# Norm statistics without transposes in a two-layer graph attention kernel

## The chip, the cores and the metric

The kernel runs on one core of one Trainium2 chip. The metric is the device time of one execution in microseconds (us); the times of the kernel before are the median, the lowest and the highest of three runs. Profiles come from one further execution each, whose own time is given beside the span of its profile.

## The reference, cut to what matters

64 graphs of 256 tokens with 512 features and a dense 256 x 256 weight matrix `adj` each go through three attentions, one after the other. All of it is float32.

```python
# layer 0: 8 heads
Q, K, V = x @ W_q + b_q, x @ W_k + b_k, x @ W_v + b_v
scores = QK/8 + a[:, :, None] + c[:, None, :] + log(adj + 1e-9)   # a, c = x @ w_g halves
x = softmax(scores) @ V + x
# layer 1, twice: 8 heads with W1, then 1 head with W2
y = (x - mean) * rsqrt(var + 1e-6) * g + b                        # the layer norm
h = y @ W;  s, t = h @ a_src, h @ a_dst
e = leaky_relu(s[:, None] + t[None, :], 0.2) + adj
x = softmax(e) @ h + x
```

The two layer norms need, for every token, the mean and the variance over its 512 features. That is what the change touches.

## The kernel before

**Layout.** One graph is one chain of some 40 steps. Its activations stand turned: `xT`, `yT` and `zT` are tiles of 128 partitions x 4 chunks x 256 tokens, so that the features of a token lie along the partitions and the chunks. `xT` is the input, `yT` the result of the first attention (with its residual), `zT` that of the second. The norm is folded into the weights (`fold_norm`): the mean is taken out of W1 and W2 beforehand, and only the factor 1/sqrt(var + eps), `rstd`, is applied per token, as TensorE's products are evicted (L607, L614, L616).

**The steps of a graph**, by the names that the order lists use:

- "load": DMA of X (L454, four pieces) and A. "turn": VectorE turns X into `xT` by 32 x 32 blocks (L471), and `adj` into AT; GpSimd forms four sums of quarters of `xT` (`left_factors`, L282 to L285, tile S); `xT` is stored to DRAM.
- "V", "V7", "V4", "Q", "Q7", "Q4", "K", "K7", "K4": a product of two 2 x 2 blocked matrices with seven block products instead of eight (`winograd`, L306 and L313). Banks a, b, c of PSUM are refilled: a product on a used bank waits for the eviction of what was in it (ScalarE L495, L528, L607; VectorE L507, L537, L545, L616).
- "scores": QK (L562) and the exponential on ScalarE (L569). "mask": VectorE multiplies by AT (L583) and adds two halves (L588).
- "sums 0": TensorE sums the weights with 32-column strips (L362), VectorE takes the reciprocal (L368), it goes to DRAM and comes back spread over the partitions as R (L376). "product 0": weights times V (L394). "gather 0": VectorE multiplies by R (L403) and adds bias and residual (L408), which gives `yT`; GpSimd forms S from it.
- "tokens 1": the statistics of `yT`, see below. "V1", "V1 7", "V1 4": the product with W1. "rows 1": the rows for the second attention go through DRAM and come back as R (L433, L443).
- "weights", eight times: ScalarE L647, VectorE L650; then the total L655. "sums 1", "product 1", "gather 1": as above, and give `zT`.
- "tokens 2": the statistics of `zT`, and the residual: X2, `zT` turned back so that tokens lie along the partitions, plus a row of biases (GpSimd L669). "V2", "V2 7", "V2 4", "rows 2", "weights 2" (L694, L699), "product 2" twice (L711, L716, L718), and the result goes to `out` (L727).

**The statistics (`tokens`, `rstd_of`).** For each half of 128 tokens TensorE transposes four 128 x 128 blocks into one bank of PSUM (L249). ScalarE reads it with Identity and adds it up (L264), scales the total by -1/512 (L265), and squares the difference, adding up again (L266). VectorE turns the sum of squares into the variance (L270), and GpSimd raises it to -1/2 (L272):

```python
for t, pt in tokens(xT):                      # 4 transposes on TensorE per half
    nc.scalar.activation(to, pt, AF.Identity, accum_out=total[:, of])
    nc.scalar.mul(less[:, of], total[:, of], -1.0 / D)
    nc.scalar.activation(pt, pt, AF.Square, bias=less[:, of], accum_out=squares[:, of])
```

For `zT` the first pass of ScalarE writes not into PSUM but into X2, which is how the residual gets turned.

**What sets the order.** TensorE's order is written out by hand: the list `period` has 42 steps, each with the age of the graph that it belongs to, so six graphs are under way at once; the lists `start` and `finish` replace the first and the last repetitions. The order of the emitted steps is TensorE's program order. The other engines' instructions are placed by a scheduler that sees the same steps; once placed, each engine works through its row in order, and so does SP, which issues nearly all DMAs. Tiles come from pools: PSUM is a ring of eight banks, ET (the weights) has four buffers, S of `yT` and of `zT` share one buffer ("yS"), X has one.

**The weights' preparation.** `fold_norm` multiplies W1 and W2 with the attention vectors on GpSimd (L177, tile `product`, which takes ET buffers) and adds up on VectorE (L181), during the first graphs.

## Time and profile before

| | us |
|---|---|
| median of three runs (lowest, highest) | 3304.04 (3301.4, 3307.49) |
| the profiled execution, its own time | 3304.79 |
| span of its profile | 3303.0 |
| TensorE matmul busy | 3208.0 |
| TensorE weight load busy | 2686.9 |
| VectorE busy | 2488.2 |
| ScalarE busy | 1761.0 |
| GpSimd busy | 899.5 |
| ScalarE's squares, L266, and their reads | 165.8 and 49.9 |
| ScalarE's first pass, L264, both forms, and its reads | 150.2 and 49.8 |
| ScalarE's scaling, L265 | 43.5 |
| TensorE's transposes, L249, all forms | 137.4 |

How to read it: PE is TensorE's matmul, PEld its weight load, DVE VectorE, ACT ScalarE, POOL GpSimd, SP the engine that issues DMAs. Busy times of a group are the union of its instructions; matmuls are pipelined and overlap, so the price of a group of matmuls is better read from the distance between the starts of two groups in the timeline than from its length. A float32 product is recorded as two matmuls, a transpose as one. A line of the timeline has the start, the length, the engine, the source line, the operation with the tile written and the tiles read, and the number of merged instructions. A line of the waits has who waited, for whom, the total, the number and the longest, in us. The granted clock of TensorE was 0.991 of full speed over the span.

### The profile page before, as it was taken

The page shows a single profiled execution, that of the slowest core. Times are in us where ns is not written, and L with a number is a line of the kernel's source. Part 1 is how long each engine was busy: PE and PEld are TensorE (multiplying, and loading weights), DVE is VectorE, ACT ScalarE, POOL GpSimd, SP SyncE. Part 2 cuts the span into 40 slices and gives each one's busy share as a digit, 9 for nine tenths or more (in the row PEclk, how much of TensorE's full clock was granted, in tenths as well). Part 3 has the DMA queues.
Part 4 walks back from the last instruction along what each step waited for, and adds up shares of the span by engine and source line. Part 5 has one row for each costly group of instructions (what it writes and reads, how often), then busy time and mean ns, then how long its engine had stood idle before and what let it go on. Part 6 is the DMA issues. An engine that isn't in the chain of part 4 may idle for free.

```text
span 3303.0 us, 76975 instructions
## 1 busy us (share of the span) xinstructions
PE 3208.0 (97%) x29000; PEld 2686.9 (81%) x29000; DVE 2488.2 (75%) x5267; ACT 1761.0 (53%) x4807; POOL 899.5 (27%) x1244
## 2 busy tenths in 40 slices
PE   6899999999999999999999999999999999999997
PEld 4688888888888888888888888888888888888875
DVE  4667777777777777787777777777777777777775
ACT  2455555555555555555555555555555555555553
POOL 2222222322322322322322322322222222222222
PEclk8999999999999999999999999999999999999998
DMA  4324333333333333343343343343343333333322
GB/s 121 105 80 112 106 97 104 109 103 104 106 107 103 105 108 103 97 115 102 98 116 101 97 112 104 93 116 104 93 118 100 98 113 105 98 107 110 99 91 69
DMA packets 271656, 340.91 MB, mean 103 GB/s; under 512 B 108577, under 2 KB 187569, under 8 KB 271281
## 3 DMA queue, kind: packets, MB, share of 16 engines
q1 hardware_dynamic: 270512, 335.40, 36.1%
q8 instruction: 232, 3.80, 0.5%
q14 instruction: 144, 1.17, 0.1%
q10 hardware_dynamic: 768, 0.54, 0.1%
HBM read 233.48 MB, written 102.31 MB: 102 GB/s over the span
## 4 chain that ended last, share of the span: by engine, by line
PE 80%; ACT 10%; DVE 3%; DMA 3%; issue 2%; SPq 1%; POOL 1%; ACTq 0%; DVEq 0%; POOLq 0%
PE ps_a L306 18%; PE ps_num L394 12%; PE ps_a L313 10%; PE ps_b L306 9%; PE ps_sc L562 7%; PE ps_av L711 6%; ACT ET L647 6%; PE ps_c L306 4%; PE ps_su L362 4%; PE ps_b L313 3%; PE ps_tr L249 3%; ACT m L528 2%; DMA R<-kept 2%; PE ps_c L313 2%; ACT u L528 1%
## 5 line engine op out<-in xcount | busy, mean ns | idle before, releaser
L650 DVE SCALAR_TENSOR_TENSOR ET<-R,f,ET 128x256 f32<-128x256 f32 x1024 | 468.3, 496 | 243.4 <-ACT ET L647 214.7
L647 ACT ACTIVATE ET<-AT,lift 128x256 f32<-128x256 f32 x1024 | 442.6, 505 | 172.0 <-PE ps_num L394 172.0
L394 PE MATMUL ps_num<-ET,V 128*32 128x256 f32 x8192 | 466.6, 380 | 0.0
L394 PEld LDWEIGHTS ps_num<-ET,V 128*32 128x32 f32 x8192 | 264.0, 110 | 155.1 <-issue 1.3
L583 DVE TENSOR_TENSOR ET<-ET,AT 128x1024 f32<-128x1024 f32 x256 | 305.2, 1227 | 112.3 <-ACT ET L569 112.3
L569 ACT ACTIVATE ET<-ps_sc,V 128x512 f32<-128x512 f32 x512 | 303.1, 702 | 101.5 <-PE ps_sc L562 90.2
L380 POOL TENSOR_TENSOR added<-added,inverse 128x128 f32<-128x128 f32 x128 | 60.1, 470 | 891.7 <-DVE inverse L368 891.7
L306 PE MATMUL ps_a<-w,S 128*128 128x264 f32 (+1 forms) x1024 | 278.6, 395 | 9.0 <-ACT m L607 8.7
L306 PE MATMUL ps_b<-w,S 128*128 128x264 f32 (+1 forms) x1024 | 267.0, 383 | 0.1
L711 PE MATMUL ps_av<-V,ET 128*128 128x258 f32 (+1 forms) x1024 | 246.6, 385 | 5.7 <-DVE ET L699 5.7
L306 PEld LDWEIGHTS ps_a<-w,S 128*128 128x128 f32 x1024 | 183.4, 190 | 71.9 <-ACT m L607 24.8
L562 PE MATMUL ps_sc<-QT,KT 64*128 64x256 f32 x2048 | 240.0, 384 | 0.0
L562 PEld LDWEIGHTS ps_sc<-QT,KT 64*128 64x128 f32 x2048 | 193.7, 188 | 41.5 <-issue 20.9
L282 POOL TENSOR_TENSOR S<-yT 128x256 f32<-128x256 f32 x64 | 54.5, 851 | 626.2 <-PE ps_su L362 556.9
L306 PEld LDWEIGHTS ps_b<-w,S 128*128 128x128 f32 x1024 | 193.9, 189 | 31.5 <-issue 0.5
L711 PEld LDWEIGHTS ps_av<-V,ET 128*128 128x128 f32 x1024 | 187.1, 193 | 29.1 <-issue 4.6
L272 POOL TENSOR_TENSOR rstd<-var,mhalf 128x2 f32<-128x2 f32 x128 | 90.6, 708 | 284.7 <-DVE var L270 278.2
L282 POOL TENSOR_TENSOR S<-zT 128x256 f32<-128x256 f32 x63 | 45.8, 727 | 445.5 <-DVE zT L408 419.2
L403 DVE TENSOR_TENSOR ps_num<-ps_num,R 128x512 f32<-128x512 f32 x256 | 165.1, 690 | 1.7 <-DMA R<-kept 1.0
L266 ACT ACTIVATE ps_tr<-ps_tr,less 128x512 f32<-128x512 f32 x256 | 165.8, 648 | 0.1
L306 PE MATMUL ps_a<-wv,xT 128*128 128x257 f32 x512 | 142.2, 400 | 22.0 <-ACT ET L569 11.6
L669 POOL TENSOR_TENSOR X<-X,bw 128x512 f32<-128x512 f32 x128 | 159.6, 1267 | 5.7 <-ACT X L264 5.7
(167 smaller groups left out, 7022.8 us busy)
## 6 DMA issues: line engine op xcount, KB each, us to landing
R<-kept SPq DMA_DIRECT2D x128, 512.0 KB
X<-in_x_dram SPq DMA_DIRECT2D x256, 128.0 KB
kept<-xT SPq DMA_DIRECT2D x64, 512.0 KB
yT<-kept SPq DMA_DIRECT2D x64, 512.0 KB
R<-kept SPq DMA_DIRECT2D x512, 64.0 KB
kept<-yT SPq DMA_DIRECT2D x64, 512.0 KB
out_dram<-X SPq DMA_DIRECT2D x512, 64.0 KB
zT<-kept SPq DMA_DIRECT2D x63, 512.0 KB
```

Of the source, the lines that this page charges most:

```text
L266: nc.scalar.activation(pt, pt, AF.Square, bias=less[:, of], accum_out=squares[:, of])
L306: nc.tensor.matmul(to, A[:, kk, :], B[:, kk, :], start=(first and kk == 0), stop=(kk == 1), skip_group_check=not first,)
L313: nc.tensor.matmul(to[:, m * P : (m + 1) * P], B[:, kk, m * P : (m + 1) * P], A[:, kk, :], start=(first and m == kk == 0), stop=(kk == 1), ...
L394: nc.tensor.matmul(num[32 * a : 32 * a + 32, m * N : (m + 1) * N], V[:, j, a // 2, a % 2 * P + q * DH + 32 * m :][:, :32], pair[a // 2][:, ...
L403: nc.vector.tensor_tensor(both, both, R[:, q, :].unsqueeze(1).to_broadcast([P, 2, N]), ALU.mult)
L562: nc.tensor.matmul(banks[h % 2][:, o : o + N], KT[lo : lo + DH, (q + h) // 2, j * P : (j + 1) * P], QT[lo : lo + DH, (q + h) // 2, :], sta ...
L569: nc.scalar.activation(ET[:, j, i::2, :], banks[i].rearrange("p (h n) -> p h n", n=N), AF.Exp, bias=c[:, j, :],)
L583: nc.vector.tensor_tensor(ET[:, j, :, :], ET[:, j, :, :], AT[:, j, :].unsqueeze(1).to_broadcast([P, 4, N]), ALU.mult,)
L647: nc.scalar.activation(ET[:, j, h, :], AT[:, j, :], AF.Exp, bias=lift[:, j, at : at + 1])
L650: nc.vector.scalar_tensor_tensor(ET[:, j, h, :], R[q][:, h, :], f[:, j, at : at + 1], ET[:, j, h, :], ALU.max, ALU.mult,)
L669: nc.gpsimd.tensor_tensor(X2[t], X2[t], folded["2"].row, ALU.add)
L711: nc.tensor.matmul(av[:, :width], ET[:, j, t * P : (t + 1) * P], V2[:, j, n, :width], start=(j == 0), stop=(j == NT - 1),)
```

## The change

Three things are changed together.

1. The statistics no longer go through transposes. ScalarE squares the whole tile (`squares_of`), GpSimd adds the four chunks of the squares and of the values in two steps each, and TensorE multiplies with a tile of ones, four 32-column strips of 128 partitions, so that sums over the partitions come out; VectorE turns them by 32 x 32 blocks, and computes the variance from the sum and the sum of squares. A tile `skew` keeps a measure of how much the two cancel, checked once at the end. The squares use the buffer of S before S is formed.
2. The residual X2 is turned by VectorE (tile Z, in the buffer of X), stored to DRAM and read back in eight pieces; then GpSimd adds the row as before.
3. The lists `period`, `start` and `finish` are new. `product` of `fold_norm` moves from the buffers of ET to those of R, `sums` and `bad` to those of "kept", and half of the loads of W_q go to ScalarE's queue.

```diff
-        def tokens(xT):
-            for t in range(NT):
-                pt = ps("tr")
-                for kc in range(KC):
-                    nc.tensor.transpose(
-                        pt[:, kc * P : (kc + 1) * P], xT[:, kc, t * P : (t + 1) * P], ident
-                    )
-                yield t, pt
...
+        def squares_of(xT, tag):
+            S = data.tile([P, 4, 2, P], F32, name="S", tag=tag)
+            wide = S.rearrange("p i k n -> p (i k n)").rearrange("p (k n) -> p k n", k=KC)
+            sums = small.tile([P, 2, N], F32, name="sums", tag="stats", bufs=1)
+            nc.scalar.activation(wide, xT, AF.Square)
+            for i, (v, half) in enumerate(((xT, wide[:, 2:]), (wide, wide[:, :2]))):
+                if i == 0:
+                    nc.gpsimd.tensor_tensor(wide[:, :2], wide[:, :2], wide[:, 2:], ALU.add)
+                    nc.gpsimd.tensor_tensor(half, v[:, :2], v[:, 2:], ALU.add)
+                nc.gpsimd.tensor_tensor(sums[:, i], half[:, 0], half[:, 1], ALU.add)
+            return S, sums
...
+        def rstd_of(sums, n):
+            pt = ps("st")
+            for g in range(4):
+                nc.tensor.matmul(
+                    pt[32 * g : 32 * g + 32, :P], all_ones,
+                    sums.rearrange("p i (t g r) -> p g i t r", t=NT, g=4)[:, g],
+                    start=True, stop=True,
+                )
+            turned = small.tile([P, 2, NT, 32], F32, name="turned", tag="turned", bufs=1)
+            nc.vector.transpose(turned.rearrange("p i t r -> p (i t r)"), pt[:, :P])
+            total, squares = turned[:, 0, :, 0], turned[:, 1, :, 0]
+            square = small.tile([P, NT], F32, name="square", tag="square")
+            nc.vector.tensor_tensor(square, total, total, ALU.mult)
             var = small.tile([P, NT], F32, name="var", tag="var")
-            nc.vector.tensor_scalar(var, squares, 1.0 / D, 1e-6, ALU.mult, ALU.add)
+            nc.vector.scalar_tensor_tensor(var, square, -1.0 / D, squares, ALU.mult, ALU.add)
+            nc.vector.scalar_tensor_tensor(skew[:, n], var, -16.0 * D, square, ALU.mult, ALU.add)
+            nc.vector.tensor_scalar(var, var, 1.0 / D, 1e-6, ALU.mult, ALU.add)
             rstd = small.tile([P, NT], F32, name="rstd", tag="rstd")
             nc.gpsimd.tensor_tensor(rstd, var, mhalf.to_broadcast([P, NT]), ALU.pow)
...
-            left = left_factors(xT, "yS")
+            S, sums = squares_of(xT, "yS")
+            left = left_factors(xT, "yS", S)
             stored = store(xT)
             yield
-            rstd = rstd_of(xT)
+            rstd = rstd_of(sums, b)
...
-            X2 = [
-                data.tile([P, D], F32, name="X2", tag="X2", bufs=4) for t in range(NT)
-            ]
-            rstd = rstd_of(xT, lambda t: by_chunk(X2[t]))
+            rstd = rstd_of(sums, B + b)
+            Z = data.tile([P, 2 * KC, P], F32, name="Z", tag="X")
+            nc.vector.transpose(
+                Z.rearrange("p b (k r) -> p k b r", k=KC), xT.rearrange("p k (b r) -> p k b r", r=32)
+            )
+            kept = dram.tile([P, 2 * KC, P], F32, name="kept", tag="keptz")
+            nc.sync.dma_start(out=kept, in_=Z)
+            X2 = data.tile([P, NT, D], F32, name="X2", tag="X2", bufs=2)
+            for q in range(4):
+                for t in range(NT):
+                    nc.sync.dma_start(
+                        out=X2[32 * q : 32 * q + 32, t, :].rearrange("r (a f) -> r a f", a=4),
+                        in_=kept.rearrange("(a r) (t q) f -> t q r a f", a=4, t=NT)[t, q],
+                    )
...
         period = [
-            (2, "rows 1"), (1, "mask"), (0, "V"), (0, "V7"), (4, "V2 4"), (1, "sums 0"),
-            (2, "weights"), (1, "product 0"), (1, "gather 0"), (4, "rows 2"), (4, "weights 2"),
-            (0, "V4"), (3, "weights"), (0, "Q"), (3, "weights"), (0, "Q7"), (3, "sums 1"),
-            (3, "product 1"), (2, "weights"), (2, "weights"), (-1, "load"), (1, "tokens 1"),
-            (0, "Q4"), (3, "gather 1"), (4, "product 2"), (2, "weights"), (1, "V1"), (2, "weights"),
-            (-1, "turn"), (1, "V1 7"), (0, "K"), (3, "tokens 2"), (0, "K7"), (4, "product 2"),
-            (0, "K4"), (1, "V1 4"), (2, "weights"), (3, "V2"), (0, "scores"), (0, "scores"),
-            (3, "V2 7"), (0, "mask"),
+            (4, "tokens 2"), (5, "product 2"), (1, "scores"), (0, "V"), (2, "rows 1"),
+            (1, "mask"), (3, "weights"), (4, "V2"), (0, "V7"), (3, "weights"),
+            (4, "V2 7"), (1, "mask"), (3, "weights"), (1, "sums 0"), (2, "weights"),
+            (1, "product 0"), (4, "V2 4"), (3, "weights"), (4, "rows 2"),
+            (3, "weights"), (0, "V4"), (1, "gather 0"), (0, "Q"), (3, "sums 1"),
+            (2, "weights"), (3, "product 1"), (2, "weights"), (0, "Q7"),
+            (4, "weights 2"), (-1, "load"), (4, "product 2"), (1, "tokens 1"),
+            (0, "Q4"), (1, "V1"), (-1, "turn"), (1, "V1 7"), (0, "K"), (3, "gather 1"),
+            (0, "K7"), (1, "V1 4"), (0, "K4"), (0, "scores"),
         ]
...
-            load_weight(nc.sync, wq, W_q)
+            load_weight(nc.sync, wq, W_q, range(0, 2))
+            load_weight(nc.scalar, wq, W_q, range(2, KC))
...
+        note_odd(skew.rearrange("p n t -> p (n t)"), -3.0e38, 0.0)
```

## The prediction

> **What bounds the kernel now.** I read the busy shares first, then the stretches of the run, then one repetition of the step list in the timeline, engine by engine, and last the waits of the start. The busy shares (part 1 of the page) and two stretches of 1000 us, with PE, PEld, DVE, ACT and POOL busy in that order:
>
> ```profile
> PE 3208.0 (97%) x29000; PEld 2686.9 (81%) x29000; DVE 2488.2 (75%) x5267; ACT 1761.0 (53%) x4807; POOL 899.5 (27%) x1244
> ...
> 1000.00:2000.00 1000.00, 994.17 (x9051) 836.97 (x9049) 769.07 (x1622) 549.98 (x1502) 274.99 (x382) 1.00 0.38 105
> 2000.00:3000.00 1000.00, 995.36 (x9067) 838.13 (x9068) 768.86 (x1622) 551.11 (x1503) 273.71 (x380) 1.00 0.37 104
> ```
>
> TensorE is the bound: it is idle 0.6% of the middle. Next is VectorE with 77%. TensorE's timeline gives the length of a period and the prices (start, length, then the group):
>
> ```profile
> 1504.70 1.03 PE L306 MATMUL ps_a<-wv,xT 128*128 128x257 f32 x4
> ...
> 1510.86 1.08 PE L362 MATMUL ps_su<-total,ones 128*32 128x128 f32 x32
> 1511.76 3.64 PE L394 MATMUL ps_num<-ET,V 128*32 128x256 f32 x64
> ...
> 1526.67 1.09 PE L249 MATMUL ps_tr<-ident,yT 128*128 128x128 f32 x8
> 1527.60 1.06 PE L313 MATMUL ps_a<-xT,wq 128*128 128x128 f32 x8
> ...
> 1540.08 1.04 PE L249 MATMUL ps_tr<-ident,zT 128*128 128x128 f32 x8
> 1540.96 1.06 PE L313 MATMUL ps_a<-S,wk 128*128 128x128 f32 x8
> ...
> 1554.42 1.03 PE L306 MATMUL ps_a<-wv,xT 128*128 128x257 f32 x4
> ```
>
> The same step comes back after 1554.42 - 1504.70 = 49.72 us: one graph per period. Ends overlap the next start, so a group costs the distance to the next start: 0.93 and 0.88 us for the two transposes, 0.90 for the 32 strips of L362.
>
> VectorE and GpSimd in the same period:
>
> ```profile
> 1512.40 0.92 DVE L368 RECIPROCAL inverse<-ps_su 128x128 f32<-128x128 f32 x1
> ...
> 1520.30 1.29 DVE L403 TENSOR_TENSOR ps_num<-ps_num,R 128x512 f32<-128x512 f32 x2
> 1521.50 1.65 DVE L408 SCALAR_TENSOR_TENSOR yT<-ps_num,columns,yT 128x256 f32<-128x256 f32 x4
> ...
> 1543.59 1.10 DVE L270 TENSOR_SCALAR var<-squares 128x2 f32<-128x2 f32 x1
> ...
> 1546.81 0.72 DVE L345 TENSOR_TENSOR top<-top,ends 128x32 f32<-128x32 f32 x1
> ```
> ```profile
> 1542.16 2.50 POOL L669 TENSOR_TENSOR X<-X,bw 128x512 f32<-128x512 f32 x2
> ...
> 1546.72 0.76 POOL L283 TENSOR_TENSOR S<-S,xT 128x256 f32<-128x256 f32 x1
> ```
>
> See two things. VectorE takes the reciprocal 0.6 us after the sums begin to leave TensorE, and yT is done at 1523.15, 3.5 us before its transposes: slack. And L270 on two columns takes 1.10 us, L345 0.72 (their fast instances take 0.15): each ends when the GpSimd instruction beside it ends. The start has one long idle, two links of the waits:
>
> ```profile
> ACT ET L569 <- DVE w L181: 11.3, 1, 11.3
> PE ps_a L306 <- ACT ET L569: 11.6, 1, 11.6
> ```
>
> **What the Trainium skill says.** "SBUF — State Buffer", Who interferes with whom: a VectorE instruction with two SBUF inputs and a GpSimd instruction that reads SBUF share one read port, and whichever starts second blocks until the first ends. The trace agrees (L270, L345; L699 beside L282 takes 0.96 us for 0.48). "TensorE: Matmul & The Clock Gate", Part 3: matmuls on different column strips run at once. The trace agrees: 32 strip records of L362 take 0.90 us, as 8 full-width records do. The same page, Part 1: after about 3.4 us of idleness the clock halves. The trace agrees: after 4.06 us idle at 101.49 us a group of 1.05 us takes 2.13.
>
> **The change, part by part.**
>
> *TensorE.* Out: 0.93 + 0.88 = 1.81 us per graph. In: four strip products per statistic, 8 records, a quarter of L362's 0.90 = 0.225, twice 0.45. Net -1.36, so the floor of a period is 48.36 us. If strips did not overlap they would cost 0.89 each and the gain would be nothing; I take 0.225 because L362 has the same form.
>
> *ScalarE.* Out (L264, L265, L266 with their accumulator reads): 459 us in all, 7.2 per graph. In: two Squares of 128x1024. Not in the trace; L647 (256) is 0.505, L487 (512) 0.723, so 0.22 per 256: 1.16, at most 2 x 0.72. Net -4.9; ScalarE (27 us per period) was not the bound, so this is worth nothing by itself.
>
> *VectorE.* In: one turn of 128x1024. L471 is 0.41 at 256 and 0.68 at 512, so 1.2 (1.0 to 1.4). Per statistic a 32x32 turn out of PSUM (0.24 at L430, 0.41 at L471: 0.28) and three more tiny operations, 0.1 when free and 0.2 when one waits for the last: about 0.95 net. Together +3.1: from 38.2 (77% of 49.72), of which 2.1 was waiting for GpSimd, to 41.3 before new waiting.
>
> *GpSimd.* In, per statistic: two of 128x512 at 1.27 (L669) and two of 128x256 at 0.73 (L283): 4.0 us. From 13.7 per period to 21.7.
>
> *DMA, SP.* In: one store of 512 KB and eight loads with 512-byte runs, like those of X, each holding SP some 0.43 us: 3.9 us of SP per graph. Behind them in SP's queue stand the store of a finished output and the R of the next weights, needed some 10 us later: hidden; if not, VectorE waits at L650. Every step of the period changes place, but none gains or loses a DMA except these; the load of X and A now stands after weights 2, with the turn five steps later (before: eight). Data moved rises by 67 MB on 341 at 36% busy: no bound. Z and X share one buffer, but the load of X comes 25 us later: hidden.
>
> *The new order.* Here I followed the instruction order built for the changed kernel. Between "ends" of one graph and the reciprocal of "sums 0" VectorE now has, in one row: the tiny ones with their waits and two turns of X (2.4), rows (0.2), the turn of Z (1.14), four masks and two totals at 1.14 (6.84), statistics and extremes (0.85), two outputs at 0.4 (0.8), eight weights at 0.4 and their total (4.3), six evictions at 0.34 or 0.4 (2.2): 18.7 us. In the kernel before, this row held 11.6 us of work in 15.8 us.
>
> From this grows a **closed loop**: ends, VectorE's row 18.7; reciprocal 0.9; the round of 1/sum through DRAM to R, 6.2 (before: L403 starts 7.0 after the reciprocal's end and seldom waits for R; its last load is issued 4.2 after); L403 and L408 2.9; Square 1.2; GpSimd 4.0 with one 0.43 for "added" between, 4.4; TensorE's tokens 1, Q4, V1, V1 7, K, K7, V1 4, 12.7 with 0.3 of gaps; eviction and ends 0.7. Sum 48.0, just below the floor of 48.36. So without new waits the loop is exactly hidden, and every further wait in it lengthens the period.
>
> The waits come from the shared port. GpSimd is busy through the first half of that row: S of zT, then S of xT, which can't start before VectorE has turned X, so they always meet the masks; then the two adds of X2 when their loads land. Encounters beyond those of before: masks 1 and 2, square, var, skew, extremes, then a mask and a total beside the X2 adds. Before, the met ones waited 0.55 (L345), 0.95 (L270), 0.48 (L699), 0.26 (L650): say 0.45 each, eight: 3.6 us (1.5 to 5). GpSimd's chain after yT meets five weights; L282 and L285 lost 0.13 and 0.19 each time: 0.8 (0.4 to 1.5). 48.0 + 3.6 + 0.8 = 52.4: +2.7 per period.
>
> What is late next: TensorE waits at tokens 1, and everything behind it (Q4, V1, K) waits with it.
>
> *Start and finish.* The fold's products no longer take ET buffers: -11.3, the wait shown above, if nothing else was as late; six graphs' worth of TensorE work outside the periods, 6 x 1.36 = -8; the statistics' path from yT to rstd grows from about 4.8 (transposes 1, ScalarE 2.7, the rest 1.1) to about 10.4 (Square 1.2, GpSimd 4.4 + S 2.9, products and turns 1.2, pow 0.7), exposed about twice: +10; and the check of skew stands in the tail after the last output: two compares, two maxima and two small ones, some 1.7 us by L352 (0.23 at 128 columns, so 0.37 at 256), L353 and L354. Half of wq's loads go to ScalarE's queue: the wait for wq is 0.29 us now, so nothing. Net -8.
>
> **Sum.** The lists give 64 x 42 steps, 137 of them in the new start list and 115 in the new finish, so 58 periods: 58 x 2.7 = 157. Profiled execution 3304.8 (span 3303.0 and 1.8 around it) + 157 - 8 = 3454; the median of the runs is 0.8 lower: **3453 us**.
>
> **Rivals.**
> - *TensorE stays the bound* (ends faster). VectorE and GpSimd fall into gaps of each other, as L345's second instance does (0.18 us right after a wait). Period 48.4 to 48.8: 3304 - 58 x 1.1 - 8 gives about 3232. It decides below some 1.8 us of added waits per period (49.72 and 8/58 against 48.0). For it: ScalarE is freed and the loop without waits is hidden. Against: GpSimd +58% while VectorE stands at 85%. Chance 0.24.
> - *Half of the waits*: 1.8 to 3.0 us in the loop, 3304 to 3370. Chance 0.15, of which 0.03 within 0.2%.
> - *The clock*: the stall at tokens 1 exceeds 3.4 us in one piece, V1 starts at half speed and the loop gains some 2 us more: 3453 + 58 x 2 = 3569. Against: a part of the idleness falls earlier, where V's third bank waits for an output's eviction. Chance 0.08.
> - *Strips don't overlap*: the floor returns to 49.7, under the loop's 52.4; it changes nothing in the forecast. It counts with the others.
>
> The forecast itself, 3370 to 3535, has 0.53. **Chances**: faster 0.24, within 0.2% (about what a measurement of this kernel can tell from no change) 0.03, slower 0.73. The range 3225 to 3565 leaves out part of the fastest case and most of the clock's.
>
> **What would show it.** Right: TensorE's busy share falls below 94%, its largest wait is at the new strip products for GpSimd's sums; masks (now 1.22) show a mean above 1.35; VectorE's reciprocal comes over 5 us after the sums of step 0. Wrong: TensorE at 99% in the middle with a period under 49; masks unchanged at 1.22. The strips show as 0.23 us per statistic. The start should show no 11 us gap.

## The result, and the profile after

The changed kernel takes 3578.84 us (median of 4 runs, 3577.87 to 3586.28) against 3305.45 (4 runs beside them): a ratio of the means of 1.0834, 95% interval 1.0815 to 1.0852. That is slower, as forecast, but outside the range: 126 us above the 3453 of the prediction and 14 above its upper end. The span of its profile is 3577.7 us.

The busy shares, and 1000 us of the middle (PE, PEld, DVE, ACT, POOL busy, granted clock, DMA share, GB/s):

```profile
PE 3272.2 (91%) x29000; PEld 2599.8 (73%) x29000; DVE 2950.1 (82%) x5849; ACT 1521.1 (43%) x3655; POOL 1616.2 (45%) x1757
...
1000.00:2000.00 1000.00, 934.77 (x8307) 742.31 (x8304) 838.88 (x1658) 436.30 (x1049) 455.29 (x493) 0.98 0.40 115
```

TensorE, busy for 994 of 1000 us before, is now idle for 65, and no other engine has taken its place as a full one: VectorE stands at 84%. So the bound is a chain. From the third "ends" to the 61st a period is 54.41 us, where it was 49.89: 58 x 4.52 = 262 of the 275 us by which the span grew. The third "ends" comes 20.6 us earlier than before (179.2 for 199.8), and from the 61st to VectorE's last instruction it takes 32.8 more.

Over the whole run TensorE's largest wait is that of product 2 (L731) for ET2, VectorE's weights of the last layer. The strip products, where the prediction expected the largest wait, wait for GpSimd's sums four times in all:

```profile
PE ps_av L731 <- DVE ET L719: 136.2, 63, 11.2
...
PE ps_st L264 <- POOL sums L257: 15.6, 4, 8.9
```

How this comes about, in one period: VectorE behind yT, GpSimd, and TensorE.

```profile
1518.03 2.07 DVE L659 SCALAR_TENSOR_TENSOR ET<-R,f,ET 128x256 f32<-128x256 f32 x2
1520.07 2.31 DVE L719 SCALAR_TENSOR_TENSOR ET<-R,f,AT 128x256 f32<-128x256 f32 x2
...
1524.71 0.41 DVE L545 TENSOR_TENSOR QT<-ps_a,m 128x256 f32<-128x256 f32 x1
```
```profile
1517.95 1.27 POOL L255 TENSOR_TENSOR S<-S 128x512 f32<-128x512 f32 x1 [8.68 <-ACT S L252]
...
1519.79 1.44 POOL L256 TENSOR_TENSOR S<-yT 128x512 f32<-128x512 f32 x1
1521.19 1.77 POOL L257 TENSOR_TENSOR sums<-S 128x256 f32<-128x256 f32 x2
```
```profile
1521.65 2.34 PE L731 MATMUL ps_av<-V,ET 128*128 128x258 f32 x8 [1.44 <-DVE ET L719]
1523.92 0.42 PE L264 MATMUL ps_st<-sums,all_ones 128*32 128x128 f32 x8
1525.18 1.16 PE L321 MATMUL ps_a<-xT,wq 128*128 128x128 f32 x8 [0.84 <-DVE QT L545]
...
1529.80 1.16 PE L314 MATMUL ps_a<-w,S 128*128 128x264 f32 x4 [0.79 <-ACT m L616]
```

Two weights, which follow each other every 0.40 us when nothing holds them, take 2.07 together, and the two of ET2 (L719) 2.31, while GpSimd adds beside them. The sums are done at 1522.96. The strip products start only at 1523.92, since product 2 (L731) stands ahead of them on TensorE and had to wait for ET2. Then Q4 waits 0.84 us for a bank whose eviction (L545) is queued on VectorE behind four such weights, and V1's fourth product 0.79 us for ScalarE's eviction, which lacked `rstd`.

### The profile page after: what moved, and what is told of

Its sections match the earlier page's. It is cut to its first block, busy times and chain, and to the rows that moved or that the text cites. A ratio compares the mean times of both kernels' runs of the same rounds, so it can differ in the third digit from the quotient of the medians.

```text
span 3577.7 us, 77824 instructions
## 1 busy us (share of the span) xinstructions
PE 3272.2 (91%) x29000; PEld 2599.8 (73%) x29000; DVE 2950.1 (82%) x5849; ACT 1521.1 (43%) x3655; POOL 1616.2 (45%) x1757
## 3 DMA queue, kind: packets, MB, share of 16 engines
q10 hardware_dynamic: 1152, 1.06, 0.1%
## 4 chain that ended last, share of the span: by engine, by line
DVE 44%; PE 29%; DMA 11%; issue 6%; SPq 4%; ACT 2%; POOL 2%; DVEq 0%; ACTq 0%; POOLq 0%
DVE ET L659 9%; PE ps_a L314 9%; DMA R<-kept 7%; DVE ET L591 7%; PE ps_a L321 6%; PE ps_b L321 4%; DVE ET L719 3%; PE ps_b L314 3%; DMA kept<-inverse 2%; DVE R L664 2%; DVE total L596 2%; PE ps_c L321 2%; DVE xT L479 2%; DVE X L738 2%; DVE Z L676 2%
## 5 line engine op out<-in xcount | busy, mean ns | idle before, releaser
L659 DVE SCALAR_TENSOR_TENSOR ET<-R,f,ET 128x256 f32<-128x256 f32 x1024 | 652.1, 676 | 1.2 <-ACT ET L656 1.2
L255 POOL TENSOR_TENSOR S<-S 128x512 f32<-128x512 f32 x128 | 164.5, 1285 | 1002.2 <-ACT S L252 604.2
L656 ACT ACTIVATE ET<-AT,lift 128x256 f32<-128x256 f32 x1024 | 461.2, 516 | 366.7 <-PE ps_num L402 360.5
L731 PE MATMUL ps_av<-V,ET 128*128 128x258 f32 (+1 forms) x1024 | 303.9, 438 | 141.4 <-DVE ET L719 136.2
L731 PEld LDWEIGHTS ps_av<-V,ET 128*128 128x128 f32 x1024 | 199.5, 210 | 213.8 <-POOL S L256 108.5
L591 DVE TENSOR_TENSOR ET<-ET,AT 128x1024 f32<-128x1024 f32 x256 | 339.1, 1328 | 2.6 <-ACT ET L577 2.6
L689 POOL TENSOR_TENSOR X<-X,bw 128x512 f32<-128x512 f32 x128 | 224.4, 1772 | 247.9 <-DMA X<-kept 192.9
L314 PE MATMUL ps_a<-w,S 128*128 128x264 f32 (+1 forms) x1024 | 276.2, 392 | 34.7 <-ACT m L616 32.8
L570 PE MATMUL ps_sc<-QT,KT 64*128 64x256 f32 x2048 | 257.2, 391 | 0.0
L570 PEld LDWEIGHTS ps_sc<-QT,KT 64*128 64x128 f32 x2048 | 182.9, 186 | 52.4 <-issue 20.0
L495 ACT ACTIVATE AT<-AT,eps 128x512 f32<-128x512 f32 x64 | 46.2, 722 | 375.3 <-DVE AT L479 370.1
L257 POOL TENSOR_TENSOR sums<-S 128x256 f32<-128x256 f32 x256 | 203.7, 815 | 0.0
L596 DVE TENSOR_TENSOR total<-ET 128x1024 f32<-128x1024 f32 x128 | 187.8, 1467 | 0.1
```

The costliest lines, as they stand in the source:

```text
L257: nc.gpsimd.tensor_tensor(sums[:, i], half[:, 0], half[:, 1], ALU.add)
L314: nc.tensor.matmul(to, A[:, kk, :], B[:, kk, :], start=(first and kk == 0), stop=(kk == 1), skip_group_check=not first,)
L570: nc.tensor.matmul(banks[h % 2][:, o : o + N], KT[lo : lo + DH, (q + h) // 2, j * P : (j + 1) * P], QT[lo : lo + DH, (q + h) // 2, :], sta ...
L591: nc.vector.tensor_tensor(ET[:, j, :, :], ET[:, j, :, :], AT[:, j, :].unsqueeze(1).to_broadcast([P, 4, N]), ALU.mult,)
L596: nc.vector.tensor_tensor(total, ET[:, 0], ET[:, 1], ALU.add)
L656: nc.scalar.activation(ET[:, j, h, :], AT[:, j, :], AF.Exp, bias=lift[:, j, at : at + 1])
```

## The loop in numbers

The closed loop of the prediction can be read from every trace: the marks are the end of "ends", the start and the end of the reciprocal of sums 0, the start of VectorE's multiplication by R, the end of yT, the first strip product (or transpose) of tokens 1, V1's first record, the start of V1 4's last record, and "ends" again. Means over 46 periods; "sums" and "ET2" are the ends of the last GpSimd addition and of ET2, counted from yT.

| us | row | recipr. | R | gather | yT to strips (sums, ET2) | to V1 | to V1 4 | to ends | period |
|---|---|---|---|---|---|---|---|---|---|
| prediction | 22.3 | 0.9 | 6.2 | 2.9 | 6.4 | 13.0 for both | | 0.7 | 52.4 |
| before | 15.12 | 0.92 | 7.32 | 2.85 | 3.50 | 3.56 | 15.06 | 1.55 | 49.87 |
| changed | 21.65 | 0.95 | 5.56 | 2.86 | 7.74 (6.14, 5.69) | 2.06 | 12.13 | 1.44 | 54.38 |
| before_stat1 | 15.05 | 0.92 | 7.31 | 2.85 | 6.20 (6.15, -) | 3.98 | 15.13 | 1.62 | 53.07 |
| half_adds | 20.04 | 0.95 | 6.00 | 2.85 | 6.70 (1.90, 5.09) | 1.65 | 12.17 | 1.13 | 51.48 |
| memset_adds | 20.45 | 0.95 | 5.65 | 2.85 | 7.03 (3.52, 5.35) | 1.84 | 12.20 | 1.20 | 52.16 |
| no_row_add | 20.07 | 0.95 | 6.10 | 2.85 | 7.29 (6.15, 5.69) | 2.22 | 12.41 | 1.45 | 53.34 |
| half_no_row | 18.48 | 0.95 | 7.42 | 2.85 | 6.40 (1.90, 4.85) | 1.70 | 12.23 | 1.13 | 51.15 |
| old_stats | 19.56 | 0.95 | 5.65 | 2.86 | 8.84 (-, 7.17) | 1.81 | 12.07 | 1.13 | 52.85 |
| old_stats_late_product | 20.96 | 0.96 | 5.80 | 2.85 | 5.57 (-, 7.28) | 1.92 | 12.67 | 1.13 | 51.85 |
| no_round | 19.05 | 0.95 | 5.64 | 2.86 | 11.99 (5.63, 9.30) | 1.71 | 11.38 | 1.26 | 54.83 |
| early_w2 | 21.87 | 0.95 | 5.45 | 2.86 | 7.22 (5.73, 5.45) | 3.76 | 12.40 | 1.18 | 55.67 |
| half_adds_early_w2 | 19.96 | 0.95 | 5.81 | 2.85 | 6.44 (1.90, 4.80) | 2.39 | 12.23 | 1.49 | 52.11 |
| late_product | 22.86 | 0.95 | 5.92 | 2.85 | 6.95 (6.90, 6.60) | 2.40 | 12.50 | 1.87 | 56.30 |
| vector_adds | 20.02 | 0.95 | 6.01 | 2.85 | 8.83 (-, 6.81) | 1.66 | 11.47 | 1.13 | 52.91 |
| vector_adds_late | 21.25 | 0.95 | 7.18 | 2.85 | 3.54 (-, 5.72) | 2.11 | 13.86 | 1.33 | 53.06 |

Each line adds up to its period, since the marks follow each other. The time is another matter: where a term only waits for TensorE it is no cause (7.42 for R in half_no_row).

## Experiments

In the expectations, theory 1 is the prediction's: GpSimd's reads beside VectorE, in this loop. The names are those of the table.

### Fewer additions, old statistics, no round, and half of the change alone

half_adds: the sums are formed without the two wide additions, so from half of the chunks.

```diff
-                    nc.gpsimd.tensor_tensor(wide[:, :2], wide[:, :2], wide[:, 2:], ALU.add)
-                    nc.gpsimd.tensor_tensor(half, v[:, :2], v[:, 2:], ALU.add)
-                nc.gpsimd.tensor_tensor(sums[:, i], half[:, 0], half[:, 1], ALU.add)
+                nc.gpsimd.tensor_tensor(sums[:, i], v[:, 0], v[:, 1], ALU.add)
```

> The changed kernel without the two additions of 128x512 on GpSimd per statistic; the statistics then come from half of the chunks only. Theory 1 (the statistics' chain after yT and GpSimd's share of the port lie in a closed loop that is longer than TensorE's work): the chain after the Square falls from 4.97 us to some 1.6, and the masks and weights beside it wait less; the period falls from 54.4 us to 49.5 to 50.5, so the time from 3579 to about 3330 (3300 to 3370). Rival 2 (VectorE's long row ahead of the reciprocal is the cost, GpSimd's waits are not): only the 2.5 us of the two additions leave the loop, period 51.9, 3434. Rival 4 (the strip products slow TensorE): 3579, unchanged.

Measured: 3396.97 us, ratio to before 1.0286 (1.0269 to 1.0303). 182 us are gone, more than rival 2 gives and less than theory 1. The sums came 1.90 us after yT, 4.2 earlier, but the strip products only 1.04 earlier: they then followed ET2, 1.6 us behind it. So something else stood at their side; that is the first sign of the branch that the prediction left out.

old_stats: `tokens`, `rstd_of` and X2 of the kernel before, and its buffers and loads of W_q, with `period`, `start` and `finish` of the changed one.

> The statistics and the residual as in the kernel before (transposes, three passes of ScalarE), with the new order lists of the changed kernel. Theory 1: without GpSimd's additions the loop is far below TensorE's 49.7 us per period, so about 3305 (3290 to 3330). Rival 2 (the new order of steps, which puts the reciprocal behind weights and evictions, costs by itself): period 52 or more, 3430 or more. Rival 3 (the residual's round through DRAM costs): as theory 1, since the round is gone too.

Measured: 3509.78 us, 1.0629 (1.0612 to 1.0647). Theory 1 missed by 205 us; the figures of rival 2 (a period of 52 or more, 3430 or more) came true. The row was 19.56 us, ET2 came 7.17 after yT and the transposes at 8.84; period 52.85. In VectorE's row four weights, their total and three evictions stood ahead of ET2 here, so the scheduler's row is not that of the changed kernel, and the run does not price the order alone.

no_round: no Z, no store, no eight loads.

```diff
-            kept = dram.tile([P, 2 * KC, P], F32, name="kept", tag="keptz")
-            nc.sync.dma_start(out=kept, in_=Z)
...
+            nc.sync.dma_start(out=X2, in_=x[b].rearrange("(t p) d -> p t d", p=P))
```

> The changed kernel without the turn of Z, its store and the eight loads; X2 is loaded from the input x with one DMA, so the residual of the last layer is the wrong tensor; GpSimd's row additions stay. Theory 1: only the 1.1 us of the turn and some waiting leave VectorE's row, period 54.4 to 52.9, about 3490 (3450 to 3520). Rival 3 (the round through DRAM, its ten DMAs in SP's queue and their data are what costs): period 51 or less, 3380 or less.

Measured: 3601.43 us, 1.0904 (1.0886 to 1.0923): not faster but slower than the changed kernel. Rival 3's 3380 or less did not come, nor did theory 1's 3490. The row is 2.6 us shorter, and all of it is lost again behind yT. From VectorE's row:

```profile
1529.48 3.79 DVE L659 SCALAR_TENSOR_TENSOR ET<-R,f,ET 128x256 f32<-128x256 f32 x4
...
1535.19 1.48 DVE L708 SCALAR_TENSOR_TENSOR ET<-R,f,AT 128x256 f32<-128x256 f32 x2
```

Four weights were placed ahead of ET2 again; it ends 9.30 us after yT, and the strip products start at 11.99. TensorE's clock, halved after such stalls in 42 of the 46 periods (see "Clock" below), adds to this.

before_stat1: the kernel before, with the new statistics for yT only.

> The kernel before, with its own order lists and its own statistics for zT, but the new statistics (Square, GpSimd additions, strip products) for yT alone; the measure skew is left out. Before, yT was ready 3.5 us ahead of its transposes; the path Square 1.2 and additions 4.9 in place of 0.9 of transposes adds 5.2 us to the loop: 46.2 + 5.2 = 51.4 us against TensorE's 49.0. Theory 1: about 51.4, 3305 + 58 x 1.7 = 3400 (3360 to 3440). Rival 2 (the new order is the cost, the statistics by themselves are hidden): 3265 to 3305.

Measured: 3511.33 us, 1.0635 (1.0617 to 1.0653). Half of the change alone, with the old lists, costs 209 us, 111 more than estimated. The sums came 6.15 us after yT (expected 1.2 + 4.9 = 6.1), the strip products at 6.20, and the waits name them:

```profile
PEld ps_st L294 <- POOL sums L287: 212.0, 64, 7.4
PE ps_st L294 <- POOL sums L287: 181.8, 64, 7.2
```

Where no product stands between, the GpSimd chain is the link, and its price was right. The period was 1.7 us above the estimate, because the piece up to V1 did not get shorter without the transposes (3.98 for 3.56), where the estimate took 0.9 us off it, and the loop before was 46.4 without its slack. TensorE's clock has a part in that piece: in 25 of the 46 periods it was halved for a while behind yT, and the piece took 4.74 us, in the others 3.09; their periods were 53.48 and 52.59.

### Product 2 as the link

early_w2 moves one step of `period`; half_adds_early_w2 does the same on top of half_adds.

```diff
-            (3, "weights"), (0, "V4"), (1, "gather 0"), (0, "Q"), (3, "sums 1"),
+            (3, "weights"), (0, "V4"), (1, "gather 0"), (4, "weights 2"), (0, "Q"), (3, "sums 1"),
...
-            (4, "weights 2"), (-1, "load"), (4, "product 2"), (1, "tokens 1"),
+            (-1, "load"), (4, "product 2"), (1, "tokens 1"),
```

> The changed kernel with one step moved: weights 2 of the graph four behind stands directly after gather 0, ahead of Q, sums 1 and the last weights; VectorE then forms ET2 before four weights and not between them. New theory (the closed loop runs through product 2: ET2 ends 5.69 us after yT, product 2 stands ahead of the strip products on TensorE, so these start 7.74 us after yT although GpSimd's sums are there after 6.14): ET2 comes some 3 us after yT, product 2 starts when TensorE is free (3.0), and the strip products wait for the sums alone, at about 6.4; period 54.4 - 1.3 = 53.1, about 3503 (3485 to 3525). Theory 1 as the prediction has it (the sums are what the strip products wait for): 3579, within 10.

> As the run before, and without the two additions of 128x512 per statistic on GpSimd (statistics from half of the chunks). There the sums came 1.9 us after yT and ET2 5.09 us after, so product 2 alone held the strip products at 6.7. New theory: product 2 now runs from 3.9 to 5.9 us after yT, the loop loses 0.8 us there and some 0.3 at Q4: period 51.5 to 50.4, 3397 - 58 x 1.1 = 3333 (3315 to 3355). If product 2 was not the link: 3397, within 10.

Measured: 3655.65 us, 1.1078 (1.1059 to 1.1096), and 3440.86, 1.0425 (1.0407 to 1.0442): both slower than without the move. ET2 was placed earlier and came hardly earlier, 5.45 us after yT: it waited for the load of its own row, which in the period shown landed 8.5 us after that row was turned. And the four weights now stood together ahead of Q4's eviction:

```profile
1548.08 2.10 DVE L719 SCALAR_TENSOR_TENSOR ET<-R,f,AT 128x256 f32<-128x256 f32 x2 [1.93 <-DMA R<-kept]
```
```profile
1554.71 1.16 PE L321 MATMUL ps_a<-xT,wq 128*128 128x128 f32 x8 [2.56 <-DVE QT L545]
```

The expectation looked at one waiter and not at what the move put behind it. In early_w2 the halved clock adds to it, in 26 of 46 periods (56.04 us for 55.08 in the others).

old_stats_late_product and late_product move product 2 from ahead of tokens 1 to behind K4.

```diff
-            (4, "weights 2"), (-1, "load"), (4, "product 2"), (1, "tokens 1"),
+            (4, "weights 2"), (-1, "load"), (1, "tokens 1"),
...
-            (0, "K7"), (1, "V1 4"), (0, "K4"), (0, "scores"),
+            (0, "K7"), (1, "V1 4"), (0, "K4"), (4, "product 2"), (0, "scores"),
```

> The old statistics with the new lists, and the first product 2 of a period moved from ahead of tokens 1 to behind K4. In the run with the old statistics ET2 came 7.17 us after yT, since four weights, a total and three evictions stood ahead of it in VectorE's row, and held the transposes at 8.84. New theory: without product 2 ahead the transposes start when TensorE is free, 5.5 us after yT or sooner, the loop falls to 49.5 or below and TensorE's 49.7 us bind: 3305 to 3340. Rival 2 (the 19.6 us row ahead of the reciprocal is what costs): 3450 or more.

Measured: 3445.86 us, 1.0437 (1.042 to 1.0455). The transposes start 5.57 us after yT and not 8.84, as TensorE comes free; that part is right. But 3305 to 3340 is not reached, and rival 2's 3450 is near: V1 stands directly behind tokens 1 in the new list, and TensorE waits 1.03 us there for evictions that lack `rstd`, whose old path (transposes, three passes of ScalarE) is longer than the work between. The two evictions of product 2 lengthened the row by 1.4.

> The changed kernel with the first product 2 of a period moved from ahead of tokens 1 to behind K4, so that the strip products no longer stand behind it on TensorE. Theory with product 2 as the link: the strip products start when the sums are there, 6.3 to 6.5 us after yT and not 7.74, and Q4 no longer waits for QT (2.06 to about 1.3 up to V1): 2.1 us out of the loop. But the two evictions of that product move into VectorE's row ahead of the reciprocal (1.2 us) and three weights move ahead of gather 0 (0.8 us). Period 54.0, 3556 (3520 to 3590). If the sums were the link already: 7.74 stays, and the row's 1.2 us make it slower: 3640.

Measured: 3688.97 us, 1.1171 (1.1154 to 1.1188), 133 us above the estimate. The link is as expected: the strip products follow the sums by 0.05 us. But the sums came later (6.90), and the stall, in two or three pieces before, was now one:

```profile
1512.57 0.53 PE L264 MATMUL ps_st<-sums,all_ones 128*32 128x128 f32 x8 [4.35 <-POOL sums L257]
1513.02 2.08 PE L321 MATMUL ps_a<-xT,wq 128*128 128x128 f32 x8
1514.89 1.69 PE L314 MATMUL ps_a<-w,yT 128*128 128x264 f32 x4
```

Q4 takes 2.08 us where 1.06 is usual, V1's first product 1.69 for 1.05; the granted clock of these 5.5 us is 0.69. This is the clock of the prediction's third rival, here in every period, for 5.1 us on the average; in the changed kernel it comes in about half of the periods.

### What GpSimd reads, and its row additions

memset_adds: fills in the place of the two wide additions; VectorE's row has the same order as in the changed kernel.

```diff
-                    nc.gpsimd.tensor_tensor(wide[:, :2], wide[:, :2], wide[:, 2:], ALU.add)
-                    nc.gpsimd.tensor_tensor(half, v[:, :2], v[:, 2:], ALU.add)
+                    nc.gpsimd.memset(wide[:, :2], 1.0)
+                    nc.gpsimd.memset(half, 0.0)
```

> The changed kernel with the two additions of 128x512 per statistic replaced by GpSimd fills of the same two regions with a constant (so the statistics are constants): GpSimd still runs two instructions in the same places of the same rows, but they read nothing. No trace has a fill of this size. Theory 1 (VectorE waits because GpSimd reads SBUF at the same time): VectorE's row falls from 21.65 to 20.0 to 20.8 as it does where the additions are missing, and the weights beside the chain after yT get shorter, whatever the fills last; if they last as long as the additions, the period is about 52.6 and the time 3475 (3440 to 3505); if they are shorter, down to the 3397 of the run without them. Rival (GpSimd's length counts, not what it reads): the row stays at 21.6 and the period shrinks by no more than what the fills are shorter than the additions.

Measured: 3434.47 us, 1.0392 (1.0376 to 1.0408). A fill took 0.526 us where an addition takes 1.28 and more. The row fell to 20.45: the three tiny operations after "ends" took 0.83 us and not 1.93, since GpSimd's additions, which still stand beside them, met only the first of them (lift, L646: still 0.63 us for 0.17). Behind yT the two weights ahead of ET2 fell from 1.98 to 0.79 us, though GpSimd worked beside them. Their group, in the changed kernel and here (busy, mean ns):

```profile
L659 DVE SCALAR_TENSOR_TENSOR ET<-R,f,ET 128x256 f32<-128x256 f32 x1024 | 652.1, 676 | 1.2 <-ACT ET L656 1.2
```
```profile
L659 DVE SCALAR_TENSOR_TENSOR ET<-R,f,ET 128x256 f32<-128x256 f32 x1024 | 533.6, 561 | 46.4 <-ACT ET L656 45.6 <-DMA R<-kept 0.8
L256 POOL MEMSET S<- 128x512 f32 x128 | 67.3, 526 | 0.0
```

That reads and not presence count is what the Trainium skill says in "SBUF — State Buffer", Who interferes with whom: a VectorE instruction with two SBUF inputs contends with a GpSimd instruction that reads SBUF, not with one that only writes it. The run agrees for these weights: the 59 that met only fills have records of 0.47 us, as undisturbed ones do. There is one reservation for the time of the run: the fills are also shorter. ET2 still came at 5.35, as it now waited 1.6 us, on VectorE's row, for its load.

no_row_add: without the two additions of L689. half_no_row: half_adds and no_row_add together.

```diff
-            for t in range(NT):
-                nc.gpsimd.tensor_tensor(X2[:, t, :], X2[:, t, :], folded["2"].row, ALU.add)
```

> The changed kernel without GpSimd's two row additions to X2 (the row of biases is left out of the residual of the last layer). Theory 1: they meet a mask and a total in VectorE's row (masks 1.33 and totals 1.47 us on the average where 1.22 is the undisturbed time); the row falls from 21.65 to about 20.3, all of it in the loop: 3579 - 58 x 1.3 = 3504 (3480 to 3535). Rival (VectorE's waits for GpSimd cost nothing, the row's length comes from its work): 3579, within 15.

Measured: 3506.81 us, 1.0623 (1.0605 to 1.0641): 72 us less, 75 expected. The totals (L596) return from 1467 to 1215 ns, the row's eight weights from 4.15 to 3.15 us. The row is 1.6 shorter, R 0.5 longer.

> The changed kernel without the two additions of 128x512 per statistic and without the two row additions to X2 (statistics from half of the chunks, the bias row of the last residual left out). The two edits alone gave 182 and 72 us. New theory: both shorten the same loop, the row by another 1.6 us with 0.5 given back by the round of R; period 51.5 - 1.1 = 50.4, 3397 - 58 x 1.1 = 3333 (3310 to 3350). Rival (TensorE's own work binds from 51 us on): 3397, within 15.

Measured: 3374.23 us, 1.0215 (1.0199 to 1.023); 41 us above the expectation and 23 below the rival's. The two edits alone gave 182 and 72, together 205. The row lost its 1.6 us, but R now took 7.42: ahead of the multiplication by R in VectorE's row stands an eviction of Q (L542 there), for which it waited 1.9 us for TensorE. TensorE was at work in 49.97 of 51.15 us; it has become the bound again, but for waits of 1.2 us.

### The additions on VectorE

vector_adds: `nc.vector` for `nc.gpsimd` in the three additions of `squares_of`; vector_adds_late: product 2 behind K4 as well.

> The changed kernel with the chunk additions of the statistics on VectorE instead of GpSimd. VectorE gets four additions per statistic, 2 x 0.68 + 2 x 0.41 = 2.2 us; those of zT fall ahead of the evictions of K, before the loop's row begins, and those of yT ahead of ET2. Theory 1 with product 2 as the link: row 19.5, reciprocal 0.95, R 5.8, gather 2.9, strip products 7.6 after yT (ET2 is later by the additions, but its weights wait for nobody), 1.2 to V1, 12.1, 1.1: 51.1, so 3579 - 58 x 3.3 = 3390 (3340 to 3450). Rival (VectorE's load is the bound, 4.4 us more of it makes it slower): 3600 or more.

> Both edits together: chunk additions on VectorE, and product 2 behind K4. With the additions on VectorE alone ET2 came 6.81 us after yT and held the strip products at 8.83. Theory with product 2 as the link: the sums come 3.8 us after yT, the strip products at 4.2, 1.2 to V1; row 20.0 + 1.2, reciprocal 0.95, R 6.0, gather 2.85, V1 and K 12.0, ends 1.1: 49.5, so that TensorE binds at about 50: 3579 - 58 x 4.4 = 3324 (3305 to 3360). If VectorE's load of the row is what costs: 3460 or more.

Measured: 3489.7 us, 1.0564 (1.0547 to 1.058), and 3500.2, 1.0599 (1.0583 to 1.0615). Both missed, by 100 and 176 us. In the first ET2 came at 6.81 and product 2 held the strip products until 8.83. In the second they started at 3.54, earlier than expected, and the gain was gone one step on: 13.86 us from V1 to V1 4 for 12.0, as the small operations of the variance stood between weights in VectorE's row and `rstd` was late (TensorE's wait there: 1.7 us), and Q4 waited for QT in half of the periods. The halved clock came in 12 of 46 periods (54.64 us for 52.40). The rival (VectorE's load costs) had 3460 or more for the second run, which came true; its 3600 or more for the first did not.

### A start that is better than both

before_product is the kernel before with one line of the change; before_fold also has two fold steps later in `start`.

```diff
-                    product = work.tile([P, 2, 2, HD], F32, name="product", tag="ET", bufs=4)
+                    product = data.tile([P, 2, 2, HD], F32, name="product", tag="R", bufs=3)
...
-            (1, "V7"), ("w1", "columns"), (1, "V4"), (0, "sums 0"), (0, "product 0"),
-            (0, "gather 0"), (1, "Q"), (1, "Q7"), ("w1", "totals"), (1, "Q4"), (0, "tokens 1"),
+            (1, "V7"), (1, "V4"), (0, "sums 0"), (0, "product 0"),
+            (0, "gather 0"), (1, "Q"), ("w1", "columns"), (1, "Q7"), (1, "Q4"), (0, "tokens 1"),
```

(The step "totals" follows K of graph 1.)

> The kernel before with one line of the change: product of the weights' folding takes the buffers of R and not those of ET. In the start ScalarE's exponential waited 11.3 us for such a buffer and TensorE 11.6 us behind it. If nothing else was as late: 3304 - 11 = 3293 (3289 to 3297). Rival (the fold's sums on VectorE or another wait take its place): 3302, within 3.

Measured: 3299.92 us (21 runs), 0.9991 (0.9985 to 0.9998). The wait of 11.6 us is gone, but only 2 of the 11 us are gained: TensorE now waits for the fold's sums and for yT.

```profile
51.84 1.04 PE L193 MATMUL ps_fold<-w,left 128*32 128x264 f32 x2 [3.18 <-DMA yT<-kept]
53.99 1.10 PE L193 MATMUL ps_fold<-w,left 128*32 128x264 f32 x6 [1.11 <-DVE w L181]
...
78.00 1.44 PE L249 MATMUL ps_tr<-ident,yT 128*128 128x128 f32 x8 [3.31 <-DVE yT L408]
```

> The kernel before with the fold's product in the buffers of R, and two steps of the start list later: columns of w1 behind Q of graph 1, totals of w1 behind K of graph 1. With the buffers alone TensorE waited 3.2, 1.1, 1.2 and 1.2 us for the fold's sums in the place of the 11.6 us. If these hide behind V4, sums 0, product 0 and Q: 3300 - 6 = 3294 (3289 to 3298). If the weights W1 are then late for V1 of graph 0: 3300 or more.

Measured: 3298.44 us (21 runs), 0.9986 (0.998 to 0.9993). This is the fastest version here, 3.6 us below the kernel before. Beyond before_product it gains 1.5 us by the medians, which the intervals don't separate.

## Why the prediction was right or wrong, point by point

**TensorE's floor**: too low. Transposes took 1.80 us per period, the strip products take 0.83 and not 0.45: their eight records need 0.35 to 0.42 us. In half_no_row, with few stalls left and no halved clock, TensorE's records still fill 49.97 us, against 49.60 before; product 2 (3.99 for 3.47), V (6.60 for 6.17) and the scores (3.86 for 3.65) have grown in the new order, for a reason that was not looked for. No run with these lists came near 48.36.

**ScalarE**: 240 us less busy, where 4.9 us per graph would be 314. Its load was no bound before or after, as said; its late evictions are another matter (V1's fourth product below).

**VectorE's row and the shared port**: the mechanism and the sum were right, 21.65 for 22.3; the parts were not, so the closeness is in part luck. The row's waits can be taken apart by the variants' times: masks 4.93 for 4.56 us (four of 1.14), weights 4.15 for 3.15, totals 2.79 for 2.27, the three tiny ones after "ends" 1.93 for 0.36, `square` 0.34, of which 0.27 is waiting: 3.7 us in all. The prediction had 3.6 on top of a row of 18.7, in which the tiny ones stood with their waits already. It named both of two masks, `var`, skew and extremes, which hardly waited, and not the eight weights, which did. And L270, which it gives as agreeing with the rule of two SBUF inputs, reads one tensor only, as lift does: that these wait too (lift 0.63 us for 0.17, L270 1.10 for 0.15) does not follow from that rule.

**Reciprocal, R, gather**: 9.37 for 10.0; R came 0.6 us sooner than taken.

**GpSimd's chain after yT**: right, 6.14 for 6.4; but it is not what the strip products wait for.

**The failed step** is the loop's next one, "Square 1.2; GpSimd 4.4; TensorE's tokens 1, Q4, V1 ... 12.7 with 0.3 of gaps", with "0.8" for what GpSimd's chain meets. It priced what the weights cost GpSimd, and not what GpSimd costs the weights, nor who stands behind them. Measured from yT to "ends" are 23.37 us, predicted 20.1. Up to the strip products it is 7.74 for 6.4: product 2, ahead of them on TensorE, holds them 1.6 us beyond the sums, as it waits for ET2 (its two halves take 1.94 us for 0.8, two weights ahead of it 1.98 for 0.79, and it waits 0.4 us on the average for its load). Part of the 1.6 is the clock, below: it is 1.0 in the periods at full clock and 2.2 in the others. From there to "ends" it is 15.63 for 13.7: 0.9 up to V1 (Q4's wait for QT behind more weights, 0.44 on the average, the longer strips, and Q4 at half clock), 0.7 at V1's fourth product, for `rstd` (two distances of 1.53 and 0.99 for 0.89), and 0.3 between V1 4 and "ends". With the 1.3 us gained above, the period is 2.0 longer than predicted, as the table says. Of these 2.0 the clock accounts for some 0.3. That product 2 is a link of its own shows in nine of the variants: the strip products come 1.5 to 2.7 us after ET2, wherever the sums are (1.90 to 6.15 us after yT where GpSimd forms them).

**Size of the misses**: against the forecast +2.7 the period grew by 4.52, 58 x 1.8 = 105 us (1.8 and not 2.0, as the prediction took the old period from one repetition, 49.72, and the mean was 49.87); the start and the finish give the other 21.

**Start and finish**: -8 forecast, +13 measured. The start gave more than was counted, -20.6 up to the third "ends"; -11.3 stood for the buffers of the product, which by themselves give 2 (before_product), so a gain was rightly forecast and its reason was not. Nor does the new start list give it alone: in old_stats, with that list but the old statistics, buffers and loads, the third "ends" comes at 201.4. Up to there the clock was halved for 34.1 us before and in old_stats, and for 13.7 in the changed kernel. The rest was not taken apart. The finish was wrong: from the last "ends" of layer 1's first attention to VectorE's last instruction 82.9 us for 60.4. In old_stats, which has the new lists and the old statistics, it is 78.8: 18 of the 22.5 us come with the new lists even without the new statistics, and the prediction did not read the finish list.

**The signs**: TensorE's share did fall below 94% (91), and the start has no gap of 11 us. The others failed: the largest wait is product 2's for ET2, the masks' mean is 1.33 and not above 1.35, the reciprocal comes 4.2 us after the sums begin and not over 5, and the strips take 0.42 us and not 0.23.

**DMA and SP hidden**: right in the main: no_round, though with another row on VectorE, gains nothing. But ET2, for which product 2 waits, waited for its own load in 34 of the graphs, 26.8 us in all, where it did so once before, for 2.0.

**Clock**: missed. The prediction gave it a chance of 0.08 and only for a stall of over 3.4 us in one piece. In the changed kernel shorter stalls were enough: in 22 of the 46 periods the clock was halved for 3.4 or 6.8 us behind yT, before in none. One of them, with a stall of 1.55 us; the stretches show the clock in the third figure from the end:

```profile
1138.40:1141.80 3.40, 1.75 (x10) 1.13 (x9) 3.40 (x4) 0.00 (x0) 3.40 (x5) 1.00 0.73 241
1141.80:1145.20 3.40, 3.40 (x18) 2.19 (x17) 3.40 (x7) 0.72 (x1) 3.32 (x4) 0.51 0.29 58
```
```profile
1140.44 3.14 PE L731 MATMUL ps_av<-V,ET 128*128 128x258 f32 x8 [1.55 <-DVE ET L719]
1143.52 0.66 PE L264 MATMUL ps_st<-sums,all_ones 128*32 128x128 f32 x8
1144.10 1.69 PE L321 MATMUL ps_a<-xT,wq 128*128 128x128 f32 x8
```

Product 2, the strips and Q4 run slowly there: the strip products start 8.37 us after yT, for 7.15 in the other periods. Most of it is caught up again, since Q4 and V1 then wait less: 54.72 us per period for 54.10, or 0.3 on the average, some 17 us of the run. So the clock is a part of the miss and not its main cause.

**What stays open**: how much the new order costs by itself. Of the 276 us, the new statistics of yT in the old lists cost 209 (before_stat1), and the new lists with the old statistics 207 (old_stats), so the two don't add up. The variants with other statistics got another row on VectorE from the scheduler, and early_w2, late_product and vector_adds_late each removed one wait and met the next, in VectorE's row behind yT or, in late_product, in one long stall for the sums. The whole change with the old lists was not tried: Z takes the buffer of X, which those lists fill again before Z would be stored.

## What to carry to other kernels

A step that leaves TensorE for GpSimd costs twice: its length enters the chain, and VectorE's instructions beside it grow, above all those with two SBUF inputs; so list, for each such instruction, who waits for it and who stands behind that waiter on an in-order engine, not only where the new result is needed. When several branches of nearly the same length meet (here sums, ET2, QT and `rstd`), shortening one of them can give little or even cost: the edits of the changed kernel that paid took reads away from GpSimd (182, 144 and 72 us, and 89 with the additions on VectorE), and moving one step in its lists did not. And an order written for a pipeline is part of the change: read the start and the finish as closely as the period. Add up TensorE's idleness over some 3.4 us and not only its longest stall.

## What the runs showed that was not expected

- A VectorE weight, 0.47 us in its record when undisturbed, takes 0.94 beside GpSimd's additions, twice its length, again and again (0.67 to 1.48 in the period shown at the top): in these stretches of the timeline the two engines take turns, one instruction each.
- GpSimd's fill of 128x512 takes 0.526 us and leaves VectorE's weights at 0.47.
- Four strip products on 32 columns each, two records each, take 0.35 to 0.42 us at full clock, not a quarter of the 0.90 that 32 such records take in a row.
- TensorE's clock does not need 3.4 us of idleness in one piece to halve. "TensorE: Matmul & The Clock Gate", Part 1, of the Trainium skill lets it halve after an idle window of about 3.4 us; the traces differ, and they decide. The halved stretches begin on a fixed grid of 3.41 us. Over the traces of all versions, in the part from 400 to 3150 us, the clock was halved after each of the 202 grid windows at full clock in which TensorE was at work for less than 1.5 us, and after none of some 13,000 with more than 1.81; between the two it went either way. So a stall of 1.55 us can be enough, and one of 2.42, which the grid cuts in two, need not be (both in the changed kernel).
